# Two-layer graph network in float32: a written instruction order for four engines in layer 1, four memory pools, and gates in the first pairs

## The chip, the cores and the metric

The kernel runs on one core of one Trainium2 chip. The core has five engines that run side by side, each with one instruction stream that it takes in order: PE (matrix multiply, with a separate row PEld for the loads of its stationary operand), DVE (vector), ACT (scalar and table functions), POOL (GpSimd) and SP (Sync, which here only issues transfers). Transfers run on 16 DMA engines. SBUF is the working memory of 128 partitions; PSUM holds the results of matmuls in eight banks of 128 x 512 float32.

The metric is the time of one execution on the device in microseconds (us), the median of repeated runs. Lower is better. All data and all matmuls are float32.

## The reference, cut to what matters

The input is 128 graphs of 128 nodes with 512 features (`x`), a dense weighted adjacency matrix for each graph, and a node mask.

```python
# layer 0
h = relu(layernorm(x))
Xw = h @ Wv + bv
sj, si = Xw @ aw[:d, 0], Xw @ aw[d:, 0]
e = leaky_relu(sj[:, None, :] + si[:, :, None] + ab, 0.2)
t = adj * exp(e);  t = t / (sum(t, -1) + 1e-12)
H = h @ Wk[0] + bk[0] + (t @ h) @ Wk[1] + bk[1] + (t @ t @ h) @ Wk[2] + bk[2]
x = x + relu(H)
# layer 1
h = relu(layernorm(x))
q, k = split(h @ Wqk);  v = h @ Wv1
agg = adj @ (k * mask)
w = mask / sqrt(512) * sum(q * agg, -1)
x = x + softmax(w, over the 128 nodes)[:, :, None] * v
```

## The kernel before

**Layer 0** goes over 64 pairs of graphs. The products with 512 x 512 weights are done by Strassen's scheme with seven instead of eight block products (`strassen`): a left operand in four blocks and four sums of them (`left_sums`, tile `sx`), a right operand prepared once (`combine`). For a pair p, `y10(p)` makes the products with the first two weights in banks a1, b1, c1, e1; `inner(p)` and `outer(p, z)` multiply by the transition matrix `t` (through a copy `zz`); `y2(p + 2)` makes the third product two pairs ahead in the other four banks. Beside them run, for other pairs, the layer norm (`norm0`, `norm2`, with a logarithm and an exponential on ACT and five small DVE operations that end in `rs`), the transposition of h through DRAM (`by_blocks`, `transposed`), and the attention (`attention`, which makes `z`, `t` and the transposed adjacency `aT`). For layer 1, `for_layer1` writes the transposed h to DRAM (`xd`), and `norm2`, `outer` and `attention` write h (`h2d`), x (`x1d`) and the adjacency (`atd`). In pairs 3 to 9, `prepare` makes layer 1's right factors and writes them to DRAM (`rwd`).

**Layer 1** goes over 32 quads of graphs (two pairs). q·agg is turned into h times one matrix, so that layer 1 needs a 512 x 1024 product of each node; it is done by Strassen's scheme twice over: an outer level with the seven factors 1 to 7, and in each of them an inner level of seven products, 49 products of 128 x 128 by 128 x 256 for a quad. The left factors of the outer level are tile `f`: four blocks loaded from `xd` (`load_left`), three of which are also summed, and four sums on POOL. The inner sums are tile `in`, made by DVE (`inner_sums`: first 0 to 3 of the factors, then the last three). `one_round` makes the seven products of one to three factors in a set of four banks; its seven steps p1, p5, p6, p2, p7, p3, p4 depend on one another through ACT's copies between banks. A quad is two calls of `together`, each with one round in set 1 and one in set 2: factors 1, 5 and 2, 6 in the first, 3, 7 and 4 in the second. Between the two, `aggregate` multiplies the adjacency (`at`) by h into banks a1, a2, e1, e2, and ACT copies the result to `agg`.

The results go to tile `c` (four blocks of a quad, three buffers) through `plain_ends` and `adding_ends`; an adding end has a DVE add from PSUM into `s` and a POOL add from `s` into `c` (L737). Two wider POOL adds (128 x 1024, L832 in the middle and L851 at the end of a quad) finish the outer level. Then `scores` multiplies `agg` by one block of `c` and sums (DVE, L795); `spread_scores` sends the scores through DRAM so that every partition has them (`pwt`, `pwd`, `pw`); one quad later `peaks`, `exps` and `factors` make the softmax and `scale` (ACT, L83) applies it; and two quads later `store` adds x with an accumulating transfer on the POOL queue (`c<-x1d`, L805) and writes the output on the Sync queue (L806).

**What sets the order.** The program is traced as Python; a scheduler then orders the instructions of each engine by priority and by its own estimate of when they can start, and places the waits. `tc.issue_after(ins)` puts what is traced in its block behind `ins` on the engine of `ins`; `behind(name, op, ...)` does that with the last instruction kept under a name in `done`. In the kernel before, PE's order is written out fully (`ordered`), and a few others are tied to such names. A tile that takes the memory of an older one waits until its readers are done; pools opened later take the memory of pools that were closed. At the change of layers the pools of layer 0 are closed, and one pool (`back`) takes their place:

```python
    layer0.close()

    back = ctx.enter_context(tc.tile_pool(name="back", bufs=1))
    fpools[1] = back
    C, W, PW, S = {}, {}, {}, {}
```

The first quad's h, adjacency and last three right factors are then loaded by ACT's queue (`load_rest(0, nc.scalar)` and L670). In a quad, the loads of the next h and adjacency (`load_rest`, L663 and L664) are traced after the stores of two quads ago, and the loads of the left factors for two quads ahead (`load_left`, L618) at the end of the quad.

Of the kernel before, what the change touches and what calls it, by code (L numbers as in the profile page):

```python
# [15 lines left out]
def kernel(  # L16
# [25 lines left out]
    nc = tc.nc  # L42
# [25 lines left out]
    loads = layer0.enter_context(tc.tile_pool(name="loads", bufs=4))  # L68
    front = layer0.enter_context(tc.tile_pool(name="front", bufs=2))
# [261 lines left out]
    def left_sums(hT):  # L331
# [3 lines left out]
        s = front.tile([P, 4, HC * N], FP, name="sx", bufs=3)  # L335
# [7 lines left out]
    def strassen(banks, left, right, s, first, ends, steps={}):  # L343
# [20 lines left out]
        done["u2"] = nc.scalar.copy(c, b).ins  # L364
# [15 lines left out]
    def begin(p):  # L380
        hT = front.tile([P, G, DC, N], FP, name="x", bufs=3)
        transposed(HV.pop(p), hT)
        LEFT[p] = left_sums(hT)
# [33 lines left out]
    def attention(p):  # L417
# [6 lines left out]
        nc.scalar.activation(z, z, AF.Exp)  # L424
# [37 lines left out]
    def y10(p, steps):  # L462
# [3 lines left out]
        def end12(b, t):  # L466
# [6 lines left out]
            (1, 0): lambda c: None}, steps)  # L473
# [48 lines left out]
    hT0 = front.tile([P, G, DC, N], FP, name="x", bufs=3)  # L522
# [28 lines left out]
    for p in range(NP):  # L551
        def lefts():
            if p == 0:
                behind("t", norm0, 2)
                behind("rs", begin, 1)
                return
            if p + 2 < NP:
                behind("t", begin, p + 2)
            if p + 3 < NP:
                behind("left", norm0, p + 3)  # L560
# [3 lines left out]
        y10(p, {1: lefts, 6: lambda: t_transposed(p)})  # L564
# [8 lines left out]
        if p == 0:  # L573
            begin(2)
            norm0(3)
# [13 lines left out]
        if p == 2:  # L589
            rightl = combine({(kh, k): rl[:, kh * HC:(kh + 1) * HC, k] for kh in range(2)  # L590
                              for k in range(2)}, [tl[:, i] for i in range(4)])
        if 3 <= p < 3 + len(FACTORS):
            prepare(FACTORS[p - 3], stage)
# [19 lines left out]
    def load_left(q, pool):  # L613
        f = F[q] = pool.tile([P, 8, G, HC, N], FP, name="f")
        fv = f.rearrange("p o j k n -> p o (j k n)")
        for o, p, kh in ((1, 2 * q, 0), (2, 2 * q, 1), (L21, 2 * q + 1, 0), (4, 2 * q + 1, 1)):
            at = L21 if o == L21 else SLOT[o]
            nc.sync.dma_start(fv[:, at], XD[p][kh].rearrange("p g n -> p (g n)"))  # L618
        at = {o: fv[:, i] for o, i in SLOT.items()}
        nc.gpsimd.tensor_add(at[5], fv[:, L21], at[4])  # L620
        nc.gpsimd.tensor_sub(at[6], at[5], at[1])  # L621
        nc.gpsimd.tensor_sub(at[3], at[2], at[6])
        nc.gpsimd.tensor_sub(at[7], at[1], fv[:, L21])  # L623

    def inner_sums(q, pool, first, n):

        v = F[q][:, first:first + n]
        s = pool.tile([P, 4, n, N], FP, name=f"in{first}")
        b = {(j, k): v[:, :, j, k] for j in range(G) for k in range(2)}
        nc.vector.tensor_add(s[:, 0], b[1, 0], b[1, 1])  # L630
        nc.vector.tensor_sub(s[:, 1], s[:, 0], b[0, 0])
        nc.vector.tensor_sub(s[:, 2], b[0, 0], b[1, 0])
        nc.vector.tensor_sub(s[:, 3], b[0, 1], s[:, 1])
        for i in range(n):
            IN[q, FACTORS[first + i]] = s[:, :, i]

# [6 lines left out]
    fpools = [early, None]  # L643
    load_left(0, early)
    inner_sums(0, early, 0, 4)
    layer0.close()

    back = ctx.enter_context(tc.tile_pool(name="back", bufs=1))
    fpools[1] = back
    C, W, PW, S = {}, {}, {}, {}  # L650

    def begin_quad(q):

        S[q] = [back.tile([P, 2, D], FP, name=f"s{i}", bufs=1) for i in (1, 2)]
        C[q] = back.tile([P, 4, G, 2, HD], FP, name="c", bufs=3)
        W[q] = wcols[q % 3]

    def load_rest(q, queue=nc.sync):
        H2[q] = back.tile([P, 2, G, D], FP, name="h2", bufs=2)
        AT[q] = back.tile([P, 2, G, N], FP, name="at", bufs=2)  # L660
        for i in range(2):
            p = 2 * q + i
            queue.dma_start(H2[q][:, i], H2D[p].rearrange("g n d -> n g d"))  # L663
            queue.dma_start(AT[q][:, i], ATD[p])  # L664

    load_rest(0, nc.scalar)
    begin_quad(0)
    for o in FACTORS[4:]:
        RW[o] = back.tile([P, 7, HD], FP, name=f"rw{o}")
        nc.scalar.dma_start(RW[o], RWD[o])  # L670

    def copy(to, at):
        done["copy"] = nc.scalar.copy(to, at).ins  # L673
# [46 lines left out]
    def plain_ends(to):  # L720

        return {(0, 0): lambda a: copy(to(0, 0), a),
                (1, 1): lambda e, t: nc.vector.tensor_add(to(1, 1), e, t),
                (0, 1): lambda b, t: nc.vector.tensor_add(to(0, 1), b, t),
                (1, 0): lambda c: copy(to(1, 0), c)}

    def adding_ends(to, other, engine=nc.gpsimd):

        def one(i, j):
            def end(a):  # L730
                done["end"] = nc.vector.tensor_add(to(i, j), a, other(i, j)).ins  # L731
            return end

        def two(i, j):
            def end(e, t):
                nc.vector.tensor_add(t, e, t)  # L736
                engine.tensor_add(to(i, j), t, other(i, j))  # L737
# [14 lines left out]
    def peaks(w, pw):  # L752
# [4 lines left out]
        nc.vector.tensor_reduce(peak, pw, AX.X, OP.max, negate=True)  # L757
        return w, pw, peak

    def exps(w, pw, peak, at, graphs):  # L760
        for j in graphs:
            ej = back.tile([P, N], FP, name="ej", bufs=2)
            behind("copy", nc.scalar.activation, ej, pw[:, j, :], AF.Exp,
                   bias=peak[:, j:j + 1], accum_out=w[:, 2, at + j:at + j + 1])

    def factors(w, pw, peak, at):
        v = w[:, :, at:at + pw.shape[1]]
        nc.vector.tensor_add(v[:, 3], v[:, 0], peak)
        behind("copy", nc.scalar.activation, v[:, 4], v[:, 3], AF.Exp)
        nc.vector.reciprocal(v[:, 5], v[:, 2])  # L770
        nc.vector.tensor_mul(v[:, 3], v[:, 4], v[:, 5])
# [198 lines left out]
```

## Time and profile before

| | before |
|---|---|
| median of 3 runs | 2424.51 us (2423.55 to 2425.39) |
| span of the profiled execution | 2428.1 us |
| mean granted PE clock | 0.982 |
| one pair of layer 0, steady (start to start of the same matmul) | 22.08 us |
| layer 0 ends, layer 1's first matmul | 1484.6 us |
| first and last L832 (31 of them, one in each quad but the last) | 1521.4 and 2376.4 us |
| `c<-x1d`, issue to landing, median | 6.7 us |
| `f<-xd`, issue to landing, median | 4.9 us |

How to read it: a busy share is an average over stages with different limits. The span is cut into 40 slices of 60.7 us; a digit is the busy share of an engine in tenths. A wait is written as the engine and the line that waited, then what released it. Lines of a helper stand for all that call it: L88 is every matmul, L83 everything issued through `behind`, L673 ACT's copies in layer 1.

### The profile page before, as it was taken

Reading aid. Unit: us, or ns where it says so; the run is one execution under the profiler, and the core shown is the slowest. Engines: PE = TensorE matmul, PEld = TensorE weight load, DVE = VectorE, ACT = ScalarE, POOL = GpSimd, SP = SyncE. Lnnn points to the kernel's source line nnn. Section 1 sums busy time; section 2 is a strip of 40 time slices with the busy share of each in tenths; the row PEclk is TensorE's granted clock in tenths of the full one; section 3 lists DMA queues with packets and bytes.
Section 4 is the critical chain, followed back from the end, with each engine's and each line's share of the span. In section 5 each row is a group of like instructions: output and inputs, shape, how many; then the busy total and the mean of one; then the engine's idle time right before and its main releaser. Section 6 shows DMA issues by size and latency. Waiting matters only on the chain.

```text
span 2428.1 us, 29205 instructions
## 1 busy us (share of the span) xinstructions
PE 2285.2 (94%) x8227; PEld 1553.5 (64%) x8227; DVE 1710.4 (70%) x4210; ACT 1259.0 (52%) x2932; POOL 865.2 (36%) x844
## 2 busy tenths in 40 slices
PE   8899989999999999999999996998989988989896
PEld 4566656665666566656665664777777767777774
DVE  5666656766666666666666663988887888888887
ACT  3455545555555555555555553555555555555554
POOL 3011111211111111111111110777767777776664
PEclk9999999999999999999999998999999999999999
DMA  7566767666666666666666655366665655666665
GB/s 199 167 194 202 228 218 206 196 189 187 199 190 182 192 200 189 186 188 200 189 186 188 201 159 181 116 166 167 176 176 161 171 157 157 168 171 167 168 172 149
DMA packets 378768, 440.68 MB, mean 181 GB/s; under 512 B 35226, under 2 KB 233498, under 8 KB 378606
## 3 DMA queue, kind: packets, MB, share of 16 engines
q1 hardware_dynamic: 346236, 382.67, 50.1%
q0 software_dynamic: 30960, 51.82, 12.0%
q10 hardware_dynamic: 1410, 4.33, 0.5%
q8 instruction: 65, 1.06, 0.2%
q14 instruction: 97, 0.79, 0.1%
HBM read 256.07 MB, written 182.63 MB: 181 GB/s over the span
## 4 chain that ended last, share of the span: by engine, by line
PE 65%; DMA 10%; POOL 10%; DVE 6%; issue 4%; ACT 2%; SPq 2%; POOLq 0%; ACTq 0%; DVEq 0%
PE c L88 18%; PE a L88 18%; PE b L88 18%; PE e L88 10%; DMA f<-xd 5%; DMA c<-x1d 4%; POOL c L737 3%; POOL f L621 1%; POOL f L623 1%; POOL f L620 1%; DVE junk L795 1%; POOL c L832 1%; POOL c L851 1%; SPq L618 1%; DVE c L731 1%
## 5 line engine op out<-in xcount | busy, mean ns | idle before, releaser
L108 POOL DMA_DIRECT2D agb<-in_adj_dram x256 | 148.5, 587 | 785.5 <-DVE aT L436 721.9
L88 PE MATMUL a<-r,x 128*128 128x512 f32 (+1 forms) x1024 | 375.5, 489 | 8.1 <-DVE x L320 8.0
L88 PEld LDWEIGHTS a<-r,x 128*128 128x128 f32 x1024 | 190.4, 191 | 88.0 <-issue 62.5
L737 POOL TENSOR_TENSOR c<-s,c 128x512 f32<-128x512 f32 (+1 forms) x186 | 220.9, 1201 | 61.1 <-DVE s L736 54.6
L88 PE MATMUL b<-rw,in 128*128 128x256 f32 x896 | 227.3, 395 | 11.1 <-ACT b L673 11.1
L88 PE MATMUL a<-rw,f 128*128 128x256 f32 x896 | 217.0, 382 | 3.0 <-ACT agg L673 3.0
L88 PEld LDWEIGHTS b<-rw,in 128*128 128x128 f32 x896 | 177.2, 199 | 44.2 <-ACT b L673 18.1
L88 PEld LDWEIGHTS a<-rw,f 128*128 128x128 f32 x896 | 169.1, 190 | 43.4 <-issue 12.9
L88 PE MATMUL c<-t,x 128*128 128x257 f32 (+1 forms) x512 | 192.2, 498 | 2.0 <-ACT s L368 1.6
L88 PE MATMUL b<-t,sx 128*128 128x257 f32 (+1 forms) x512 | 191.7, 497 | 1.1 <-ACT b L360 1.1
L88 PE MATMUL c<-t,sx 128*128 128x257 f32 (+1 forms) x512 | 187.5, 488 | 0.0
L88 PE MATMUL e<-t,sx 128*128 128x257 f32 (+1 forms) x512 | 187.0, 488 | 0.0
L88 PE MATMUL b<-r,sx 128*128 128x257 f32 (+1 forms) x512 | 186.3, 486 | 0.0
L88 PE MATMUL c<-rw,in 128*128 128x256 f32 x448 | 118.9, 408 | 68.1 <-ACT c L673 68.1
L320 DVE STREAM_TRANSPOSE x<-hv 128x512 f32<-128x512 f32 x254 | 165.3, 688 | 13.4 <-DMA hv<-h2d 8.7
L276 DVE BATCH_NORM_STATS2 st<-xg 128x6 f32<-128x512 f32 x128 | 82.4, 685 | 116.4 <-DMA xg<-in_x_dram 116.4
L795 DVE SCALAR_TENSOR_TENSOR junk<-agg,wscale,c 128x512 f32<-128x512 f32 x128 | 160.1, 1251 | 3.6 <-POOL c L737 2.3
L630 DVE TENSOR_TENSOR in<-f 128x512 f32<-128x512 f32 x64 | 53.5, 836 | 140.1 <-POOL f L621 137.5
L368 ACT COPY s<-c 128x257 f32<-128x257 f32 (+1 forms) x128 | 60.6, 473 | 171.0 <-PE c L88 171.0
L88 PEld LDWEIGHTS c<-t,x 128*128 128x128 f32 x512 | 92.3, 189 | 84.9 <-issue 50.2
L88 PEld LDWEIGHTS b<-t,sx 128*128 128x128 f32 x512 | 94.0, 191 | 81.6 <-issue 61.0
L88 PEld LDWEIGHTS c<-rw,in 128*128 128x128 f32 x448 | 86.3, 198 | 90.8 <-ACT c L673 79.3
(216 smaller groups left out, 4718.5 us busy)
## 6 DMA issues: line engine op xcount, KB each, us to landing
x1d<-x SPq DMA_DIRECT2D x64, 512.0 KB, 3.7
h2d<-h SPq DMA_DIRECT2D x64, 512.0 KB, 3.1
hv<-h2d SPq DMA_DIRECT2D x256, 128.0 KB, 3.6
xd<-x SPq DMA_DIRECT2D x128, 256.0 KB, 3.0
f<-xd SPq DMA_DIRECT2D x128, 256.0 KB, 4.9
xg<-in_x_dram SPq DMA_DIRECT2D x63, 512.0 KB, 4.5
hd<-h SPq DMA_DIRECT2D x63, 512.0 KB, 3.1
hv<-hd SPq DMA_DIRECT2D x252, 128.0 KB, 2.9
```

What stands on the lines that cost most here:

```text
L88: done["mm"] = op(*args, **how).ins
L108: nc.gpsimd.dma_start(agb[p][c * S32:(c + 1) * S32].rearrange("p g q i -> p (g q) i"), v[c])
L276: nc.vector.bn_stats(st, src[:, j, :])
L320: nc.vector.transpose(dst[:, j].rearrange("p f (n b) -> p f n b", n=Q), hv[:, j].rearrange("p n (f a) -> p f n a", f=Q))
L368: nc.scalar.copy(s[:, 1], c)
L618: nc.sync.dma_start(fv[:, at], XD[p][kh].rearrange("p g n -> p (g n)"))
L620: nc.gpsimd.tensor_add(at[5], fv[:, L21], at[4])
L621: nc.gpsimd.tensor_sub(at[6], at[5], at[1])
L623: nc.gpsimd.tensor_sub(at[7], at[1], fv[:, L21])
L630: nc.vector.tensor_add(s[:, 0], b[1, 0], b[1, 1])
L737: engine.tensor_add(to(i, j), t, other(i, j))
L795: nc.vector.scalar_tensor_tensor(junk, agg[:, pair, j], wscale[:, b:b + 1], y[:, j].rearrange("p h d -> p (h d)"), op0=OP.mult, op1=OP.mul ...
```

## The change

In layer 1, every instruction of Sync, POOL, DVE and ACT goes through `put`, which ties it behind the one before it on its engine; so the order in which the Python code traces them is the order in which each engine takes them. The code is then rearranged by hand. `load_left` is split in two: the loads (for the next quad, at its head, in `catch_up`) and POOL's sums (`sum_left`, in the first half of the quad before their use). `inner_sums` becomes four steps that are hung between PE's steps. The last adds, the scores and their spread move from a quad's end to the head of the next one (`catch_up`). `store` is split into the accumulating transfer (`add_x1`) and the write. `exp_own`, the exponential of the scores on a row's own partition, leaves `factors` and goes ahead of the others.

The pool `back` becomes four, so that each takes memory of layer 0 that is freed at another time; in layer 0 the tiles `x` and `sx` get a pool of their own (`lefts`). The first h, adjacency, right factors and second quad's left factors are loaded by the POOL queue instead of ACT's. In the first pairs, `norm0(3)`, `combine` of the right factor and `prepare` are put behind the last DVE operation of `outer`, and pair 0's copy c<-b of `y10` behind the exponential of `attention`.

```diff
+    lefts = layer0.enter_context(tc.tile_pool(name="lefts", bufs=3))
...
-        s = front.tile([P, 4, HC * N], FP, name="sx", bufs=3)
+        s = lefts.tile([P, 4, HC * N], FP, name="sx")
...
-        done["u2"] = nc.scalar.copy(c, b).ins
+        behind(u2, nc.scalar.copy, c, b)
...
-        nc.scalar.activation(z, z, AF.Exp)
+        done["z"] = nc.scalar.activation(z, z, AF.Exp).ins
...
-            (1, 0): lambda c: None}, steps)
+            (1, 0): lambda c: None}, steps, "warm" if p else "z")
...
-            norm0(3)
+            behind("x1", norm0, 3)
...
-            rightl = combine({(kh, k): rl[:, kh * HC:(kh + 1) * HC, k] for kh in range(2)
+            rightl = behind("x1", combine, {(kh, k): rl[:, kh * HC:(kh + 1) * HC, k] for kh in range(2)
...
-            prepare(FACTORS[p - 3], stage)
+            behind("x1", prepare, FACTORS[p - 3], stage)
...
+    def put(engine, op, *args, **how):
+
+        if engine in done:
+            with tc.issue_after(done[engine]):
+                done[engine] = op(*args, **how).ins
+        else:
+            done[engine] = op(*args, **how).ins
...
-    back = ctx.enter_context(tc.tile_pool(name="back", bufs=1))
+    back = [ctx.enter_context(tc.tile_pool(name=f"back{i}", bufs=1)) for i in range(4)]
...
-    load_rest(0, nc.scalar)
-    begin_quad(0)
-    for o in FACTORS[4:]:
-        RW[o] = back.tile([P, 7, HD], FP, name=f"rw{o}")
-        nc.scalar.dma_start(RW[o], RWD[o])
+    begin_quad(0)
+    load_rest(0, swdge)
+    for o in FACTORS[4:]:
+        RW[o] = back[1].tile([P, 7, HD], FP, name=f"rw{o}")
+        swdge(RW[o], RWD[o])
+    load_left(1, back[2], swdge)
...
+    def catch_up(q):
+
+        if q + 1 < NQ:
+            load_left(q + 1, back[2] if q % 2 == 0 else early, sync)
+
+        pool(nc.gpsimd.tensor_add, outer(q - 1, 1), outer(q - 1, 3), outer(q - 1, 1))
+        scores(q - 1, 1, C[q - 1][:, 2])
+        PW[q - 1] = spread_scores(W[q - 1])
+        if q > 1:
+            add_x1(q - 2, 0)
...
-                 {5: lambda: scale(q - 2, 1, 0), 6: lambda: scale(q - 2, 1, 1)} if q > 1 else {})
-
-        done["v"] = nc.gpsimd.tensor_add(outer[0], outer[3], outer[1]).ins
-        if q > 1:
-            behind("v", store, q - 2)
-        if q > 0:
-            late = behind("end", peaks, W[q - 1], PW.pop(q - 1)) + (0,)
-        agg = aggregate(q)
-        load_rest(q + 1)
-        inner_sums(q + 1, early, 0, 4)
+                 {0: work(*sums[:2]), 1: work(*sums[2:], lambda: sum_left(q + 1)),
+                  2: lambda: load_rest(q + 1, sync),
+                  3: (lambda: scale(late, 1, 0)) if q > 1 else nothing,
+                  5: (lambda: scale(late, 1, 1)) if q > 1 else nothing})
+        if q > 1:
+            store(late, 0)
+        if q > 0:
+            soft = peaks(W[prior], PW.pop(prior))
+
+        pool(nc.gpsimd.tensor_add, outer(q, 0), outer(q, 3), outer(q, 1))
+        if q > 1:
+            add_x1(late, 1)
+        aggregate(q)
         scores(q, 0, c[:, 2])
-
-        work = {i: lambda i=i: exps(*late, (i,)) for i in range(4)}
-        work[4] = lambda: factors(*late)
-        work.update({i: lambda i=i: scale(q - 1, 0, i - 5) for i in (5, 6)})
+        sums = inner_sums(q + 1, early, 0, 4)
+
+        hooks = {0: sums[:2], 1: sums[2:]}
+        if q > 0:
+            hooks = {0: [lambda: exp_own(*soft), lambda: exp(*soft, 0)] + sums[:2],
+                     1: [lambda: exp(*soft, 1)] + sums[2:],
...
-        nc.gpsimd.tensor_add(outer[1], outer[3], outer[1])
-        if q + 2 < NQ:
-            load_left(q + 2, fpools[q % 2])
-        inner_sums(q + 1, back, 4, 3)
-        scores(q, 1, c[:, 2])
-        PW[q] = spread_scores(W[q])
+        if q > 1:
+            store(late, 1)
+            C.pop(late)
```

## The prediction

> **What bounds the kernel now.** I read the busy line and the slices first, then the busy times by stage, then the chain of waits in layer 1, then the waits by total, and last the timeline of one quad.
>
> ```profile
> PE 2285.2 (94%) x8227; PEld 1553.5 (64%) x8227; DVE 1710.4 (70%) x4210; ACT 1259.0 (52%) x2932; POOL 865.2 (36%) x844
> ...
> PE   8899989999999999999999996998989988989896
> ...
> POOL 3011111211111111111111110777767777776664
> ```
>
> The 94% says "TensorE-bound", and for slices 3 to 24 (layer 0) that is right: a pair costs 22.08 us, all of it matmuls. The last 16 slices (layer 1) are another stage: PE falls below 90% and POOL rises from 1 to 7 tenths.
>
> ```profile
> core 0: us, PE busy (x) PEld busy (x) DVE busy (x) ACT busy (x) POOL busy (x), PEclk, DMA share, GB/s
> 1521.40:2376.40 855.00, 776.45 (x3206) 615.85 (x3204) 712.39 (x1046) 461.96 (x1045) 604.98 (x417) 0.98 0.60 163
> 1484.60:1521.40 36.80, 18.30 (x66) 13.62 (x65) 15.62 (x30) 8.78 (x17) 8.05 (x6) 0.72 0.68 246
> ```
>
> The first window runs from the first to the last of the 31 POOL adds of L832, one in each quad: 855.0/30 = 28.5 us per quad. DVE is busy 23.7 of it, POOL 20.2, ACT 15.4. A quad has 98 matmul records of 0.216 us (eight take 1.73) and 8 of 0.43: PE needs 24.6. So 3.9 us per quad are lost. The second window is the change of layers: PE worked 18.3 of 36.8 us.
>
> The chain of waits (start, length, what) repeats one loop from quad to quad:
>
> ```profile
> 1601.53 2.67 POOL c L832
> 1604.90 8.08 DMA c<-x1d
> 1616.30 4.98 DMA f<-xd
> 1630.10 2.68 POOL c L832
> ```
>
> The waits of layer 1 (total, times, longest) show how it reaches PE, and those of the Sync queue where it starts:
>
> ```profile
> POOL f L623 <- DMA f<-xd: 151.4, 23, 8.2
> DVE in L630 <- POOL f L621: 128.4, 28, 6.1
> ACT ej L83 <- DVE peak L757: 94.5, 29, 4.6
> ...
> PE c L88 <- ACT c L673: 65.3, 27, 3.7
> ...
> SPq L806 <- DMA c<-x1d: 455.3, 56, 15.7
> ```
>
> Read upwards: PE waits for a copy in ACT's queue, queued behind an exponential that waits for the peak, which DVE does after a sum that waited for POOL, which waited for the left factors `f`; their load stood in the Sync queue behind stores that wait for the accumulating transfer `c<-x1d`. One quad of POOL's timeline (start, length, and in brackets the idle time before it):
>
> ```profile
> 1802.80 2.68 POOL L832 TENSOR_TENSOR c<-c 128x1024 f32<-128x1024 f32 x1
> 1805.42 2.44 POOL L805 DMA_DIRECT2D c<-x1d  x2
> ...
> 1822.55 1.26 POOL L623 TENSOR_TENSOR f<-f 128x512 f32<-128x512 f32 x1 [6.37 <-DMA f<-xd]
> ...
> 1828.21 2.94 POOL L737 TENSOR_TENSOR c<-s,c 128x512 f32<-128x512 f32 x2
> 1831.22 2.67 POOL L832 TENSOR_TENSOR c<-c 128x1024 f32<-128x1024 f32 x1
> ```
>
> With the `f` loads issued at 1816.52 (Sync's row of the same timeline), the loop is: L832 2.6, from the x1d issue to the f issue 11.1, to the first f sum 6.0, four f sums 5.7, two L737 3.0: 28.4 us. That is the period. No engine is full; a loop through a DMA queue sets the pace.
>
> **What the Trainium skill says.** "SBUF — State Buffer", section "Who interferes with whom": a DVE instruction with two SBUF inputs and a GpSimd instruction that reads SBUF exclude each other; the later one blocks fully. The trace agrees: a 384-wide sum (L632), 0.55 us alone, took 2.70 at 1842.33, beside a POOL add of 2.66. "Perfetto Trace Analysis", section "GPSIMD Engine Instruction": GpSimd spans are unreliable, starts are to be used; hence my POOL lengths are from starts (f sums 1822.55, 1823.78, 1825.12, 1826.47). "DMA: Bandwidth & Descriptors", section "Issuing engines are not separate DMA queues": another issuing engine adds no bandwidth; at the change of layers the transfers already ran at 246 GB/s. "TensorE: Matmul & The Clock Gate", section "What's actually happening": an idle PE falls to half clock; after the 18.5 us pause there, eight matmuls took 3.78 us instead of 1.89.
>
> **The change part by part.**
>
> (1) Written order on Sync, POOL, DVE and ACT in layer 1. The four `f` loads now stand at the head of a quad. In the instruction order they still follow the second store of the quad before, which waits for its own accumulating transfer; but that is now one transfer, issued right after L832's add, and the loads of h and at no longer stand between. New loop: add 2.6, one x1d (median 6.7 from issue to landing), store issue 0.4, f issue to sum 6.0, f sums 5.7, two c adds 3.0: 24.4 us, an estimate. The old loop loses 4 us and falls to PE's 24.6.
>
> (2) What the order costs. DVE work per quad, by starts: ten 512-wide adds from PSUM at 0.6, four 256-wide at 0.36, four 384-wide sums at 0.5, four 512-wide at 0.6, four scores at 0.78, one reduction 0.6, transpose and small ones 0.7: 16.2 us. Waits in the new fixed order: the scores of pair 1 head DVE's queue at the quad's start, and wait for POOL's last c adds and then for the lock behind the 1024-wide add (L851's): 3.4. Behind them queue the spread of the scores, the 384-wide sums and the PSUM add that frees bank a2 for the aggregate. The scores of pair 0 meet the other 1024-wide add: 2.6. The factor product 0.7. The f sums, moved to the first half, run when the 384-wide sums do: nothing if f lands late, up to 4.8 if each of four sums waits for an f sum. That makes 22.9 to 27.7. Laid out in time: if f lands about 9.5 us into the quad, there is no collision, but POOL's c adds and then the scores come later, and the quad closes at 25.7; if it lands at 6.8, all four collide, DVE frees a2 some 1.5 us late, and it closes at 27.1. The scores' spread takes 7.4 us through DRAM and is back before the peak in both. I take 26.3: 2.2 us less than 28.5, times 30 quads = 66 us. Ends: 24.9 (PE with a little waiting) and 27.7.
>
> (3) ACT: exponentials now wait for a peak that DVE reaches 2 to 4 us earlier; `exp_own` moves up, which costs nothing (0.2 us, beside matmuls). ACT has 7.9 us in PE's 9.1 of the second half (four pairs of copies at 0.95, four exponentials at 0.6, two scalings at 0.73, `exp_own` 0.2), so it hides.
>
> (4) Four pools, and the first h, at and right factors by the POOL queue. Before, ACT's queue issued them and stood 19.7 us behind `h<-h2d`, which waited for layer 0's last `xd<-x`, with PE's copies behind it: PE paused 18.5 us. Now ACT has nothing to issue, and the memory of the first tiles was last read at pair 63's matmuls. But 2.7 MB of right factors, 1 MB of f and 1.3 MB of h and at must come in some 17 us, and POOL sums the second quad's f before the first quad's adds, for which ACT's second-half copy into `s` waits: I leave 5 us of new pause, and gain 12 (8 to 18).
>
> (5) Gates in the first pairs. In pairs 10, 11 and 12 (26.5, 26.4 and 25.0 us instead of 22.1) ACT has the copy of zz before the logarithm of the next norm, and DVE's add into bank e waits 5 us. In the new order only pair 10 is put right: 4.4. Pair 0's exponential moves ahead of the c copy (PE waited 3.4 for t), and the 1024-wide `combine` leaves the front of x of pair 2 (PE waited 8.0), though norms now stand there: 2.6 together. From pair 13 to the end of layer 0 no engine's order changes. Sum 7 (3 to 12).
>
> (6) The last quads: stores moved behind the work, exponentials spread out: 2. The `lefts` pool only renames memory in layer 0: nothing.
>
> Sum: 66 + 12 + 7 + 2 = 87; 2424.5 - 87 = 2337.5.
>
> **The rivals.** A: PE becomes the bound. For it: both loops can reach 24.6, and with fewer pauses the clock stays full. 24.9 per quad: 30 x 3.6 = 108, with 21 elsewhere 2295. Against it: POOL's 16.6 us of adds (8 at 1.25, 2 at 0.7, 2 at 2.6) and DVE's 7.6 us of work with two SBUF inputs (sums 4.4, scores 3.1, product 0.15) exclude each other, 24.2 us on one port. B: the lock takes the place of the load. All collisions happen: 27.7, 24 + 21 = 45 less, 2380. C: slower. A fixed order leaves no other work to fill a wait: if peaks also come 1.5 late behind the spread, 29.2 per quad, 21 lost, and the gain at the boundaries is used up by transfers that are late there: 2432.
>
> **How the numbers follow.** My forecast (25.5 to 27.2 per quad) 0.46, A 0.20, B 0.22, C 0.10, no difference 0.02. The range reaches from just below A to a quad of 28.4 with the other gains: 2290 to 2402. Faster 0.88 (forecast, A, B), same 0.02, slower 0.10.
>
> **What would show it.** Right: the period of L832's successor near 26.3; POOL's wait for f below 3 us a quad; Sync's wait for x1d still there but before f no more than 2 us; pauses of PE at the aggregate's second matmul instead of at product 7; PE's pause at the change of layers under 7 us; pair 10 at 22.1 us. Wrong: ACT's copies still the releaser of product 7 by over 2 us, POOL still waiting 5 us for f, or PE without pauses in layer 1.

## The result and the profile after

The changed kernel takes 2362.53 us in the median (2354.90 to 2370.35), against 2424.03 us; the ratio is 0.9746, with a 95% interval of 0.9713 to 0.9779. It is 61.5 us faster. Forecast were 87 us.

The page of the changed kernel, busy line and slices:

```profile
PE 2259.0 (96%) x8227; PEld 1540.4 (65%) x8227; DVE 1758.6 (75%) x4210; ACT 1258.4 (53%) x2932; POOL 838.1 (36%) x855
...
PE   8899999999999999999999999899999999999996
...
DVE  5576666766666666666666665699999999999997
POOL 3011111211111111111111111477776777767772
```

PE's slices of layer 1 are now nines, but so are DVE's. The busy times of two stretches (same columns as before), from the first to the last of the 31 POOL adds that stand where L832 stood, and the first two quads:

```profile
1497.30:2304.00 806.70, 754.07 (x3162) 600.60 (x3163) 763.43 (x1051) 458.45 (x1035) 574.07 (x417) 0.99 0.66 174
1470.57:1534.51 63.94, 54.63 (x213) 42.76 (x212) 42.41 (x69) 26.09 (x57) 32.17 (x27) 0.89 0.53 177
```

The quad takes 806.70/30 = 26.9 us instead of 28.5. DVE is busy 763.43/30 = 25.4 of them, though it has no work that it hadn't before (23.7). The waits of layer 1 (total, times, longest):

```profile
PEld a L89 <- DVE c L618: 76.1, 31, 3.2
PE a L89 <- DVE c L618: 39.2, 24, 2.4
DVE junk L618 <- POOL c L618: 39.1, 32, 13.6
...
PE c L89 <- ACT c L618: 0.9, 2, 0.5
...
POOL f L618 <- DMA f<-xd: 0.2, 1, 0.2
```

(Most instructions of layer 1 now bear L618, the line of `put`, so that tiles tell them apart.) POOL's wait for `f`, 151.4 us before, is gone; so is nearly all of PE's wait for ACT at product 7 (65.3 us before). A new wait stands in their place: PE's bank `a` waits for a DVE add. One quad of DVE's timeline shows what DVE does at that time:

```profile
1913.33 2.82 DVE L618 SCALAR_TENSOR_TENSOR junk<-agg,wscale,c 128x512 f32<-128x512 f32 x1 [0.79 <-POOL c L618]
...
1916.20 2.40 DVE L618 SCALAR_TENSOR_TENSOR junk<-agg,wscale,c 128x512 f32<-128x512 f32 x1
...
1918.78 1.37 DVE L618 TENSOR_TENSOR in<-f 128x384 f32<-128x384 f32 x1
1920.18 1.51 DVE L618 TENSOR_TENSOR in<-in,f 128x384 f32<-128x384 f32 x1
1921.61 1.61 DVE L618 TENSOR_TENSOR in<-f 128x384 f32<-128x384 f32 x1
1923.15 0.55 DVE L618 TENSOR_TENSOR in<-f,in 128x384 f32<-128x384 f32 x1
1923.62 0.68 DVE L618 TENSOR_TENSOR c<-a,c 128x512 f32<-128x512 f32 x1
```

And POOL and PE in the same time:

```profile
1913.26 2.35 POOL L618 TENSOR_TENSOR c<-c 128x1024 f32<-128x1024 f32 x1
...
1916.33 6.48 POOL L618 TENSOR_TENSOR f<-f 128x512 f32<-128x512 f32 x4
...
1924.35 1.12 PE L89 MATMUL a<-h,at 128*128 128x512 f32 x2 [2.21 <-DVE c L618]
```

The first score is blocked by the 1024-wide add, the second and three of the four 384-wide sums by POOL's `f` sums; the fourth sum runs alone and takes 0.55. (In 15 of the quads 2 to 29 the fourth is blocked too; the mean of all these sums is 1.40.) Only then comes the add from bank a2 (`c<-a,c`), and the aggregate's second matmul, which writes a2, has waited 2.2 us.

PE's idle time in quads 2 to 29 changes its place as well: 2.7 us a quad before, 2.3 of it at product 7 of the second half; 1.7 us now, nearly all at the aggregate's second matmul.

By stage, between the first matmuls of pairs and quads in the two profiles (us; pairs are counted from 0, as in the kernel and in the prediction):

| stage | before | changed | difference |
|---|---|---|---|
| up to pair 2 | 114.7 | 104.1 | -10.6 |
| pairs 2 to 8 | 154.9 | 156.4 | +1.5 |
| pairs 9 to 11 | 75.4 | 69.4 | -6.0 |
| pair 12 to the end of layer 0 | 1139.9 | 1140.6 | +0.8 |
| quads 0 and 1 | 70.5 | 63.9 | -6.6 |
| quads 2 to 29, each | 28.50 | 26.82 | -47.1 for 28 |
| quads 30, 31, end | 74.8 | 74.3 | -0.5 |

They add up to 68.5, 7 more than the medians give: the profiled execution of the kernel before took 2429.84 us, 5.8 more than its median, and that of the changed kernel 2361.39, 1.1 less. A part lies in the first row: in the profiles of experiments 7 and 8, whose layer 0 is that of before, pair 2 starts at 111.7 and 113.7 us, not at 114.7.

### The profile page after: what moved, and what is told of

Same layout as the page of the kernel before. It is cut to its first block, busy times and chain, and to the rows that moved or that the text cites. A ratio compares the mean times of both kernels' runs of the same rounds, so it can differ in the third digit from the quotient of the medians.

```text
span 2359.6 us, 29167 instructions
## 1 busy us (share of the span) xinstructions
PE 2259.0 (96%) x8227; PEld 1540.4 (65%) x8227; DVE 1758.6 (75%) x4210; ACT 1258.4 (53%) x2932; POOL 838.1 (36%) x855
## 4 chain that ended last, share of the span: by engine, by line
PE 78%; DVE 11%; DMA 4%; issue 3%; ACT 2%; POOL 2%; SPq 0%; DVEq 0%; ACTq 0%; POOLq 0%
PE a L89 23%; PE b L89 21%; PE c L89 21%; PE e L89 13%; DVE junk L618 3%; DVE in L618 2%; DVE c L618 2%; POOL c L618 1%; DVE s L618 1%; DMA pwd<-pwt 1%; DMA pw<-pwd 1%; ACT h L295 1%; DMA f<-xd 1%; DVE wcol L618 1%; DMA t<-in_L_gnn_Wv_dram 1%
## 5 line engine op out<-in xcount | busy, mean ns | idle before, releaser
L618 POOL TENSOR_TENSOR c<-s,c 128x512 f32<-128x512 f32 (+1 forms) x186 | 199.9, 1088 | 230.3 <-DVE s L618 225.4
L618 DVE SCALAR_TENSOR_TENSOR junk<-agg,wscale,c 128x512 f32<-128x512 f32 x128 | 245.8, 1920 | 44.2 <-POOL c L618 39.1
L89 PE MATMUL b<-rw,in 128*128 128x256 f32 x896 | 219.8, 385 | 0.9 <-ACT b L618 0.9
L618 POOL TENSOR_TENSOR f<-f 128x512 f32<-128x512 f32 x127 | 194.5, 1541 | 18.9 <-DMA f<-xd 13.9
L89 PEld LDWEIGHTS b<-rw,in 128*128 128x128 f32 x896 | 170.2, 192 | 29.1 <-ACT b L618 6.4
L369 ACT COPY s<-c 128x257 f32<-128x257 f32 (+1 forms) x128 | 60.6, 474 | 175.9 <-PE c L89 175.8
L618 POOL TENSOR_TENSOR c<-c 128x1024 f32<-128x1024 f32 x62 | 145.8, 2351 | 2.4
L89 PEld LDWEIGHTS e<-t,sx 128*128 128x128 f32 x512 | 97.5, 190 | 68.6 <-issue 60.0
```

The lines of the kernel that those rows point to most:

```text
L89: done["mm"] = op(*args, **how).ins
L369: nc.scalar.copy(s[:, 1], c)
L618: done[engine] = op(*args, **how).ins
```

## The experiments

**Theory and rivals.** L: what is left per quad is PE waiting for DVE's add from a2, queued behind two-input instructions that POOL blocks; another order gives most of it back. M: DVE and POOL together fill the shared port, so any order costs the same. And of the kernel before: the loop through Sync's queue (theory), or the port (rival).

**1. The sums later.** In the changed kernel, the four 384-wide sums after the last PSUM add of the first half:

```diff
-                 {0: work(*sums[:2]), 1: work(*sums[2:], lambda: sum_left(q + 1)),
+                 {1: lambda: sum_left(q + 1),
...
-                  5: (lambda: scale(late, 1, 1)) if q > 1 else nothing})
+                  5: (lambda: scale(late, 1, 1)) if q > 1 else nothing,
+                  6: work(*sums)})
```

> The changed kernel with one move in DVE's order: the four 384-wide sums of a quad's second-half factors no longer stand between the scores' transpose and the add that frees bank a2, but after the last PSUM add of the first half. POOL's order is as it was. Theory L (what is left per quad is PE waiting for DVE's add from a2, queued behind sums that are blocked by POOL's f sums): the pause of 2 to 3 us at the aggregate's second matmul goes, the sums take 0.55 us instead of 1.4, the quad falls from 26.9 to 24.8-25.5 us, in all 2305 to 2325 us. Rival M (DVE and POOL have no slack on the shared port, so whatever is moved collides elsewhere): the quad stays at 26.3 to 27.0 and the pause moves to the second half's product 5, which reads these sums; 2350 to 2365 us.

Measured: 2339.22 us, ratio 0.9645 (0.9623 to 0.9666), 26.1 us a quad. The aggregate no longer waits, but PE now waits 1.3 us a quad at product 7 of the second half. DVE's timeline of this run:

```profile
1880.84 1.45 DVE L618 TENSOR_TENSOR in<-f 128x384 f32<-128x384 f32 x1
1882.32 1.51 DVE L618 TENSOR_TENSOR in<-in,f 128x384 f32<-128x384 f32 x1
1883.75 2.70 DVE L618 TENSOR_TENSOR in<-f 128x384 f32<-128x384 f32 x1
1886.37 0.55 DVE L618 TENSOR_TENSOR in<-f,in 128x384 f32<-128x384 f32 x1
1886.84 0.67 DVE L618 TENSOR_REDUCE peak<-pw 128x4 f32<-128x512 f32 x1
```

They now meet POOL's c adds and the other 1024-wide add, and the peak, on which ACT's exponentials wait, stands behind them. Neither expectation held: 0.7 of the 1.4 to 2.1 us that L wanted were won, and M's collision came as well, though at product 7 and not at the product 5 that M named.

**2. Quad 0's order on POOL.** The `f` sums of quad 1 behind quad 0's adds, in quad 0 alone:

```diff
-                 {0: work(*sums[:2]), 1: work(*sums[2:], lambda: sum_left(q + 1)),
+                 {0: work(*sums[:2]), 1: work(*sums[2:], *([lambda: sum_left(q + 1)] if q else [])),
...
         pool(nc.gpsimd.tensor_add, outer(q, 0), outer(q, 3), outer(q, 1))
+        if q == 0:
+            sum_left(1)
```

What it mends, in the timelines of the changed kernel (POOL, then PE):

```profile
1475.40 0.54 POOL L618 DMA_DIRECT2D f<-xd  x1 [0.73 <-DMA h<-h2d]
1489.62 5.16 POOL L618 TENSOR_TENSOR f<-f 128x512 f32<-128x512 f32 x4 [13.68 <-DMA f<-xd]
1494.74 2.48 POOL L618 TENSOR_TENSOR c<-s,c 128x512 f32<-128x512 f32 x2
...
1498.17 2.93 PE L89 MATMUL c<-rw,in 128*128 128x256 f32 x6 [6.74 <-ACT c L618]
```

> The changed kernel with one move in POOL's order, in quad 0 alone: the four f sums of quad 1 stand behind quad 0's two c adds and its 1024-wide add, not ahead of them. Theory: the pause of 6.7 us at product 7 of quad 0's second half and the half clock after it come from POOL waiting 13.7 us for f's fourth load with the c adds queued behind; the pause goes and the change of layers is 6 to 8 us shorter: 2354 to 2357 us. Rival: the loads of h, at, right factors and f on POOL's DMA queue are what is late, and PE then waits for f's sums at the start of quad 1 instead: gain of 0 to 3 us, 2360 us.

Measured: 2355.14 us, ratio 0.9706 (0.9688 to 0.9724): 7.4 less than the changed kernel, though the two intervals overlap a little (that of the changed kernel begins at 0.9713). In the profiles quads 0 and 1 take 53.8 us instead of 63.9. The pause at product 7 is gone; one of 3.4 us at the start of quad 1, behind DVE's sums of the late `f`, is what the rival saw. The theory holds for the larger part: the pause was made by the order, with work queued behind one load.

**3. Without the gates of layer 0.**

```diff
-        behind(u2, nc.scalar.copy, c, b)
+        done["u2"] = nc.scalar.copy(c, b).ins
...
-            behind("x1", norm0, 3)
+            norm0(3)
...
-            rightl = behind("x1", combine, {
+            rightl = combine({
...
-            behind("x1", prepare, FACTORS[p - 3], stage)
+            prepare(FACTORS[p - 3], stage)
```

> The changed kernel without the gates in layer 0's first pairs (norms, the right factors' combination and their preparation free again, pair 0's c copy not behind the exponential); layer 1 as changed. Theory: pairs 10 and 11 go back to 26.2 to 26.7 us (they are 22.5 and 24.4 with the gates), pairs 3 to 10 gain back 0.2 each: 4 to 7 us longer, 2367 to 2370 us. Rival: the 14.3 us by which the profile of the changed kernel leads at the end of layer 0 all come from the gates: 12 to 14 us longer, 2375 us.

Measured: 2371.70 us, ratio 0.9781 (0.9763 to 0.9798), 9.2 more than with the gates; here too the intervals overlap. In the profiles pair 12 starts at 337.2 us instead of 329.9: 4.3 of these 7.3 us come before pair 2, 4.5 in pairs 10 and 11 (25.0 and 26.4 us, with the gates 22.5 and 24.4), and 1.5 go back in pairs 2 to 8, which are slower with the gates (22.3 us instead of 22.1). That is between the two expectations, nearer the first. In the kernel before, pair 12 starts at 345.0 (341.9 and 344.0 in the two kernels below that have its layer 0); so 4.7 to 7.8 us ahead of pair 12 are not the gates'. How much of that is the spread of single executions is not known; of the change only the `lefts` pool is left there, and it was not tried alone.

**4. Only Sync's order kept.**

```diff
-        if engine in done:
+        if engine in done and engine == "sync":
```

> The changed kernel with the written order of layer 1 kept on Sync's queue alone; DVE, ACT and POOL are in the order that the scheduler gives them. Theory (the gain per quad came from the f loads ahead of stores and of h and at): POOL's wait for f stays under 1 us a quad and the quad stays at or under 27.5 us: 2340 to 2385 us. Rival (the orders of DVE, ACT and POOL are what shortened the quad): the quad is back at 28 us or over, 2400 us or over, although f is there in time.

Measured: 2637.29 us, ratio 1.0870 (1.0842 to 1.0897), 36.5 us a quad: far worse than either expected. ACT and PE in one of its quads (L620 is `put` here):

```profile
1909.14 0.58 ACT L620 COPY s<-c 128x512 f32<-128x512 f32 x1 [0.85 <-PE c L89]
1918.20 0.40 ACT L620 ACTIVATE ej<-pw,peak 128x128 f32<-128x128 f32 x1 [8.48 <-DVE peak L620]
...
1918.60 0.56 ACT L620 COPY s<-c 128x512 f32<-128x512 f32 x1
```

```profile
1919.22 2.07 PE L89 MATMUL c<-rw,f 128*128 128x256 f32 x4 [6.72 <-ACT s L620]
```

The scheduler's order on ACT has an exponential ahead of the last copy that PE needs in the first half. The exponential waits for the peak (254 us in 28 quads), the peak for the spread of the scores through DRAM (107 us), and PE for the copy: 7.3 us a quad. In the kernel before, ties of `behind` keep the peak and the exponentials back; the changed kernel has no such ties, since `put` does their work, so this run is not the order of the kernel before on three engines. POOL's wait for `f` is 15.5 us in all, as the theory has it, and doesn't help: the quad is set elsewhere. What the other three orders are worth in time, against those of the kernel before, this run does not tell.

**5. The f sums on DVE.** `sum_left` with `dve(nc.vector...)` instead of `pool(nc.gpsimd...)`, put after the adds that free banks a and e:

```diff
-                 {0: work(*sums[:2]), 1: work(*sums[2:], lambda: sum_left(q + 1)),
+                 {0: work(*sums[:2]), 1: work(*sums[2:]),
...
+                  4: (lambda: sum_left(q + 1)) if q else nothing,
```

> The changed kernel with the four f sums of a quad on DVE instead of POOL: after the first adds that free the banks a and e in the first half (in quad 0 at the start of its second half). POOL then has 13.5 us of work a quad instead of 18.6, and DVE four adds of 0.7 us more. Theory L (POOL's f sums block DVE's sums and second score, and so hold back the add that frees bank a2): the four 384-wide sums take 0.55 us instead of 1.4, the aggregate's second matmul does not wait, and with quad 0's wait for f gone too the time is 30 x 1.6 + 6 lower, 2300 to 2318 us. Rival M (DVE is the fuller engine, and 2.8 us of work more on it cost what the lock gives back): the quad stays at 26.3 to 27.2 us, 2345 to 2370 us.

Measured: 2336.44 us, ratio 0.9633 (0.9619 to 0.9647), 26.4 us a quad. The lock is as L has it: the 384-wide sums take 0.54 us in the mean instead of 1.40, and PE no longer waits for DVE's add from a2. The time fits neither expectation. 8.4 of the 26 us won against the changed kernel come from quads 0 and 1 (55.5 us instead of 63.9); in the other quads DVE's further work delays what ACT waits for (ACT's own exponential waits 47.9 us in all for DVE, 3.2 in the changed kernel), and PE waits for ACT:

```profile
PE c L89 <- ACT c L618: 25.0, 15, 2.0
...
PE a L89 <- DVE c L618: 2.3, 6, 0.7
```

**6. Sync's order given up, the other three kept.**

```diff
-        if engine in done:
+        if engine in done and engine != "sync":
```

> The changed kernel with the written order kept on DVE, ACT and POOL and given up on Sync's queue, where the scheduler's own order has one out store between the two loads that spread the scores, and the h and at loads and the other store ahead of the f loads, as in the kernel before. Theory (the f loads ahead of h and at are what shortens the quad): POOL waits for f again, 1 to 4 us a quad, and the quad is at 27.5 to 29 us: 2385 to 2430 us. Rival (with the order of the accumulating transfers on POOL changed, Sync's order is worth little): 26.7 to 27.2 us a quad, 2360 to 2372 us.

Measured: 2327.95 us, ratio 0.9595 (0.9579 to 0.9611): both expectations wrong, and 35 us less than the changed kernel. POOL does wait for `f` again, but only 32 us in all, and the quad is at 25.7. POOL and DVE in one of its quads:

```profile
1896.65 2.35 POOL L618 TENSOR_TENSOR c<-c 128x1024 f32<-128x1024 f32 x1
...
1901.22 5.87 POOL L618 TENSOR_TENSOR f<-f 128x512 f32<-128x512 f32 x4 [1.09 <-DMA f<-xd]
```

```profile
1899.60 0.75 DVE L618 SCALAR_TENSOR_TENSOR junk<-agg,wscale,c 128x512 f32<-128x512 f32 x1
...
1900.53 0.52 DVE L618 TENSOR_TENSOR in<-f 128x384 f32<-128x384 f32 x1
1901.08 0.56 DVE L618 TENSOR_TENSOR in<-in,f 128x384 f32<-128x384 f32 x1
1901.55 1.63 DVE L618 TENSOR_TENSOR in<-f 128x384 f32<-128x384 f32 x1
...
1904.65 0.68 DVE L618 TENSOR_TENSOR c<-a,c 128x512 f32<-128x512 f32 x1
```

The `f` sums start 4.6 us after the 1024-wide add, not 3.1 (these are the medians of quads 2 to 29 too). In that gap DVE has the second score and two sums unblocked, and the add from a2 comes 8.0 us after the 1024-wide add starts instead of 10.4 (in the medians 8.0 and 9.9). PE's wait at the aggregate falls from 1.7 to 0.1 us a quad; 0.6 us at product 7 take its place. The gap also varies within this run: one quad with 3.5 us waits 1.1 us at the aggregate, four with 4.2 or 4.3 us wait 0.3 there, those with 4.5 or more not at all, and two with 6.2 and 6.3 us wait 1.5 us at product 7 instead (quads 2 and 25, the shortest ones, don't fit: 3.1 and 6.4 us, and hardly a wait). So here a later load makes the quad shorter, up to a point. But Sync's order moved stores, h and at too, and the 1024-wide add itself starts 0.6 us earlier in the quad (3.7 us after its first matmul, not 4.3); these were not separated.

**7. The kernel before with its stores behind the loads.** `store` is split; the accumulating transfers stay where they were, the two out stores are issued behind the last `f` load of the quad:

```diff
-            behind("v", store, q - 2)
+            behind("v", add_x1, q - 2)
...
             load_left(q + 2, fpools[q % 2])
+        if q > 1:
+            behind("f", put_out, q - 2)
```

> The kernel before, with one edit: the two out stores of a quad stand behind the four f loads in Sync's queue, not ahead of two h and at loads and of f. Nothing else of the change. Theory (the period of 28.5 us is the loop L832, x1d transfer, store, f load, f sums): the wait of f for x1d goes, POOL's wait for f (5 us a quad) falls under 1, and the quad is 25.3 to 26.8 us: 2325 to 2375 us. Rival (f late is a symptom; DVE and POOL exclude each other and set the period): 28.0 us or more a quad, 2405 us or more.

Measured: 2319.94 us, ratio 0.9560 (0.9541 to 0.9579). One edit to the kernel before brings 104 us, 43 more than the whole change. Its quads 2 to 29 (columns as above):

```profile
1552.70:2251.10 698.40, 694.46 (x2969) 561.72 (x2968) 669.06 (x980) 433.10 (x980) 578.78 (x392) 1.00 0.68 189
```

698.4/28 = 24.94 us a quad, and PE is busy in 694.5 of 698.4. Sync's queue, two lines of its timeline, and POOL's wait for `f`:

```profile
1852.77 1.84 SPq L618 DMA_DIRECT2D f<-xd  x4
1854.72 1.24 SPq L817 DMA_DIRECT2D out_dram<-c  x2
```

```profile
POOL f L623 <- DMA f<-xd: 1.4, 5, 0.4
```

With the stores behind the loads, the quad falls below what was expected, to PE. The edit leaves one other cause open: the scheduler, placing DVE's instructions anew, now has the third 512-wide sum (L632) behind the peak and not ahead of it, and in Sync's queue h and at too are free of the stores. The kernel before itself decides this. In its quad 2 no store stands ahead of the `f` loads yet, since the first one is issued at 1580.83 us, while DVE has its old order (L632, then the peak):

```profile
1555.57 1.74 SPq L618 DMA_DIRECT2D f<-xd  x4
```

```profile
1558.31 2.67 POOL L851 TENSOR_TENSOR c<-c 128x1024 f32<-128x1024 f32 x1
1560.93 1.58 POOL L623 TENSOR_TENSOR f<-f 128x512 f32<-128x512 f32 x1
```

POOL does not wait, and this quad takes 24.6 us; in the quads after it, with the stores ahead of the loads, the `f` sums come 8 to 11 us after that add instead of 2.6, and the quad takes 26.3 to 31.2 us. So the loop named in the prediction is what held the kernel before. The port does not prevent it: in this run too the 384-wide sums are blocked (1.49 us in the mean), but ahead of the scores, in the time in which DVE would wait for POOL's c adds.

**8. The kernel before with the first loads on POOL's queue.**

```diff
-    load_rest(0, nc.scalar)
+    load_rest(0, nc.gpsimd)
...
-        nc.scalar.dma_start(RW[o], RWD[o])
+        nc.gpsimd.dma_start(RW[o], RWD[o])
```

> The kernel before, with one edit: the first h and at tiles and the right factors of layer 1 are loaded by POOL's queue instead of ACT's; the memory pool stays one. Theory (ACT's copies were queued behind those issues): the pause of 18.5 us at product 7 of quad 0 falls below 10 us, quad 0 from 45.9 to 33-39 us, 2411 to 2418 us. Rival (what is late is the memory under the tiles, which one pool frees only after layer 0's last reader, so that the four pools and not the queue are what helped): PE waits as long, at the aggregate or at f's sums: 2420 to 2426 us.

Measured: 2426.71 us, ratio 1.0014 (1.0000 to 1.0028): nothing won, as the rival has it. PE's pauses in this run:

```profile
1503.54 3.78 PE L88 MATMUL c<-rw,f 128*128 128x256 f32 x8 [8.99 <-ACT s L673]
1510.73 3.19 PE L88 MATMUL a<-h,at 128*128 128x512 f32 x4 [3.42 <-issue]
...
1518.51 0.70 PE L88 MATMUL a<-rw,f 128*128 128x256 f32 x2 [1.88 <-DMA rw<-rwd]
1521.43 1.08 PE L88 MATMUL a<-rw,f 128*128 128x256 f32 x2 [2.22 <-DMA rw<-rwd]
```

Most of the 18.5 us is only spread out: 9.0 + 3.4 + 1.9 + 2.2 = 16.5, and quads 0 and 1 together take 72.0 us, 70.5 before. ACT's own copy into `s` still waits for layer 0's last `xd<-x`. That fits the rival, memory that one pool frees late; the queue alone changes nothing. That the four pools alone, with ACT's queue, would do was not tried.

**9 and 10. The sums first, and with quad 0's order.** In the changed kernel, DVE's order as the scheduler has it in experiment 7: the 384-wide sums at the head of the quad, before the scores.

```diff
             begin_quad(q)
+            for step in inner_sums(q, back[0], 4, 3):
+                step()
             catch_up(q)
-            sums = inner_sums(q, back[0], 4, 3)
+            sums = []
```

> The changed kernel with one move in DVE's order: the four 384-wide sums of a quad stand at its head, before the two scores of the quad before, not behind them. Sync, POOL and ACT as changed. Theory O (in the changed order DVE first waits for POOL's c adds with the scores at its head, and meets POOL's f sums with the sums; the order, not the amount of work, is what costs): the sums run while POOL does its c adds, the add that frees bank a2 is done 3 to 4 us earlier, the aggregate's pause goes, 25.0 to 25.8 us a quad, 2310 to 2332 us. Rival M (the shared port is full, so the sums and scores are only blocked by other POOL instructions): 26.3 to 26.9 us a quad, 2345 to 2363 us.

> The move of the sums to the head of the quad together with quad 0's order on POOL (c adds ahead of the f sums of quad 1). If the two costs are separate, 7 us below the first alone: 2303 to 2325 us. If quad 1 then waits for f, equal to it.

Measured: 2328.92 us, ratio 0.9612 (0.9596 to 0.9627), and 2323.66 us, 0.9593 (0.9571 to 0.9616). The quad is at 25.9 in both, and theory O holds in time (2310 to 2332) though the quad is just over its 25.8. The sums are blocked as before (0.97 and 2.70 us for two of them), but in time that DVE had spent waiting; that is 1 us a quad from order alone. Quad 0's order takes 8.3 us off quads 0 and 1 in the profiles (53.9 instead of 62.2); in the medians it is 5 us, and the two intervals overlap. PE's remaining waits are 0.7 us a quad at product 7 and 0.2 to 0.3 at the aggregate.

**11. The exponentials one product later**, on top of 10:

```diff
-            hooks = {0: [lambda: exp_own(*soft), lambda: exp(*soft, 0)] + sums[:2],
-                     1: [lambda: exp(*soft, 1)] + sums[2:],
-                     2: [lambda: exp(*soft, 2)],
-                     3: [lambda: exp(*soft, 3)],
+            hooks = {0: sums[:2],
+                     1: [lambda: exp_own(*soft), lambda: exp(*soft, 0)] + sums[2:],
+                     2: [lambda: exp(*soft, 1)],
+                     3: [lambda: exp(*soft, 2), lambda: exp(*soft, 3)],
```

> The two moves of the run before (sums at the head of the quad, quad 0's order) and one in ACT's order: the own exponential and the four others stand one product later in the second half, behind the copies of e, so that no copy which PE needs stands behind a wait for the peak. Theory A (what is left per quad, 25.9 against 24.9 in the kernel before with its stores moved, is ACT's written order: 0.66 us of PE's wait for ACT's copies at product 7): the wait goes and the quad is at 25.0 to 25.4 us, 2300 to 2312 us. Rival: the scores' spread arrives late (DVE waits 3 us for it) and the exponentials, moved back, push the factors and the scalings of c later, so that the copies of the next quad wait instead: 25.8 to 26.2 us a quad, 2320 to 2332 us.

Measured: 2321.84 us, ratio 0.9567 (0.9543 to 0.9591), 25.6 us a quad. The wait at product 7 falls from 0.67 to 0.06 us, but 0.26 us at product 6, which waits for ACT's copy into bank b, come in its place, as the rival said, and the time is not told apart from that of 10. What else separates 25.6 from 24.9 stays open.

**12. The best of both.** Experiment 7, and of the change only the gates, the `lefts` pool and the four memory pools with the first loads on POOL's queue; layer 1 in the scheduler's order.

```diff
-    back = ctx.enter_context(tc.tile_pool(name="back", bufs=1))
+    back = [ctx.enter_context(tc.tile_pool(name=f"back{i}", bufs=1)) for i in range(4)]
...
-    load_rest(0, nc.scalar)
     begin_quad(0)
+    load_rest(0, nc.gpsimd)
```

> The kernel before with the stores behind the f loads, and of the change only the gates in the first pairs and the four memory pools with h, at and the right factors on POOL's queue; no written order in layer 1. Stores alone gave 2319.9; the gates are worth 9 us by their own run; the boundary was 63 us over two quads in the changed kernel with quad 0's order mended to 54, and 70.5 with stores alone: 2319.9 - 9 - 7 to 16 = 2295 to 2304 us. Rival (without the written order the scheduler puts POOL's f sums of quad 1 ahead of quad 0's adds, and nothing is won at the boundary): 2308 to 2313 us.

Measured: 2301.94 us (2298.40 to 2305.20), ratio 0.9501 (0.9480 to 0.9522), 60.6 less than the changed kernel and within the expected range. The quad is at 24.88, quads 0 and 1 at 57.6 (70.5 in experiment 7); a pause of 5.7 us at product 7 of quad 0 is left, behind POOL's sums of quad 1's `f`, as the rival said, but it does not use up the gain.

## Why the prediction was right, and where it was not

**The loop** (step 1) was right. POOL's wait for `f` fell from 151.4 to 0.2 us in layer 1, and experiment 7 with quad 2 of the kernel before shows that this loop held the kernel before: 28.5 to 24.9 us a quad by moving two stores. Its new length was right too. In one quad of the changed kernel, from one middle add to the next (Sync, then POOL):

```profile
1897.35 12.54 SPq L618 DMA_DIRECT2D out_dram<-c  x2
1910.01 2.47 SPq L618 DMA_DIRECT2D f<-xd  x4
```

```profile
1901.01 2.35 POOL L618 TENSOR_TENSOR c<-c 128x1024 f32<-128x1024 f32 x1
...
1925.57 2.50 POOL L618 TENSOR_TENSOR c<-s,c 128x512 f32<-128x512 f32 x2 [2.76 <-DVE s L618]
1928.15 2.35 POOL L618 TENSOR_TENSOR c<-c 128x1024 f32<-128x1024 f32 x1
```

The adds are 27.1 us apart, and POOL spends 2.8 of it waiting for DVE: 24.4 us without that wait, the figure of step 1. One sign failed: `f` was to wait for x1d no more than 2 us, but its loads are still issued right behind a store that waits for x1d up to 12 us (306.5 us in all). It costs nothing, because POOL's sums of `f` now stand behind another add.

**The DVE order** (step 2) named the right wait, at the right instruction: the scores behind POOL's add, the sums behind the `f` sums, the aggregate's second matmul at the end. Its size was wrong, and it is the term that failed. The prediction had two layouts, 25.7 if `f` comes late and 27.1 if it comes early enough to collide, and took 26.3 between them. But step 1's loop, 24.4 us, is shorter than either layout's quad, so by step 1 the quad does not wait for `f`. Measured 26.82, with three or four of four sums blocked; over 30 quads this is 16 us of the 25 that were missing. So the colliding layout was good to 0.3 us. That experiment 6, with `f` later, is at 25.68 looks as good for the other layout, but is partly luck: the layout had `f` 9.5 us into the quad and no collision, and there the sums start at 8.4 us in the median and two of four are still blocked. Rival A (PE's bound) needs only another order: experiment 7. Rival C's figure, 2432, does not follow from its terms: 2424.5 + 21 - 7 - 2 is 2436.5 without the gain at the change of layers.

**ACT** (step 3) hides in the changed kernel: PE waits 0.9 us in all for its c copies. It is the next to show: as soon as DVE's add is early, product 7 waits for it (1.3, 0.9, 0.6 and 0.7 us a quad in experiments 1, 5, 6 and 9).

**The change of layers** (step 4) was to bring 12, and brought 6.6. Its cause was named, POOL's `f` sums ahead of the c adds, and sized at a pause of 5 us. The pause was 6.7; after it matmuls ran at half clock (six took 2.93 us instead of 1.46); and quad 1 waits for DVE's add like the others, which the 5 us had left out. With POOL's order mended (experiment 2), quads 0 and 1 are 10 us shorter in the profile, 7.4 in the medians. That ACT's issues were what held PE before is refuted as the sole cause by experiment 8.

**The gates** (step 5) came out at 7.3 against 7 forecast, by the profiles of experiment 3 and the changed kernel. That the sum agrees is luck, since the parts differ: 4.5 in pairs 10 and 11 (4.4 forecast, for pair 10 alone, which gains 2.5), 4.3 instead of 2.6 at the start, and 1.5 lost in pairs 2 to 8, which was not foreseen. The other 7.0 us that layer 0 gains between the two profiles were not forecast: the `lefts` pool was put at nothing, and whether it or the spread of single executions makes them stays open. **The tail** (step 6) brought 0.5 instead of 2.

The sum by stage with the gates' share alone is 47.1 + 6.6 + 7.3 + 0.5 = 61.5. That this is the difference of the medians is chance, as the 7.0 us are left out of it. The mechanism was right; of the 25 us that are missing, 16 are step 2's term, 5 step 4's and 1.5 the tail's.

## What to carry to other kernels

When no engine is full, find the loop that sets the period, and first move the one instruction that closes it: two stores behind four loads brought 104 us, where a written order of four engines with the same aim brought 61 together with everything else. A quad that lacks the instruction under suspicion, as quad 2 lacks the stores, is a test that the kernel makes by itself. A written order also freezes which instructions of DVE and POOL meet and block each other; put the two-input DVE work into the time in which DVE would wait for POOL anyway, and not behind that wait. And when an estimate has two layouts, decide between them from its own earlier steps instead of taking the middle.

## What was not expected of the hardware

A load that lands earlier can cost time: with POOL's `f` sums 1.5 us nearer to its 1024-wide add they meet DVE's second score and sums, and the quad was 1.1 us longer (26.82 against 25.68 in experiment 6, with what else differs there). It is not the landing as such: in quads 2 and 11 of the changed kernel POOL's add starts 2.8 us into the quad instead of 4.3 and the `f` sums at 5.9 and 6.0 instead of 7.4, and these quads take 25.0 us. All four sums are blocked there too, but the add from a2 is reached 12.6 us into the quad instead of 14.1, and PE waits 0.2 us at the aggregate. What counts is how late DVE is for PE's next use of the bank.

Short waits of PE cost more than their length. Over quads 2 to 29 the records have PE's clock at half for 37.5 us in the kernel before, 10.2 in the changed one and 0 in experiment 7, whose longest pause of PE there is 0.7 us. Each stretch is 3.4 us long and follows a single pause of 2.1 to 3.7 us. In the changed kernel ten of these quads pause 2.2 us at the aggregate: three of them, each with such a stretch, take 28.8 us, and the other seven 27.15. In the kernel before the half clock costs 0.7 us a quad, an estimate (37.5/2/28), beyond the waits that the profile lists.

The fourth `f` load on POOL's queue, behind 4.8 MB of others issued there within 8 us (h and at 1.3, right factors 2.75, f 0.77), let POOL wait until 14.2 us after its issue; on Sync's queue the median of these loads is 4.1 us. Most of this is not the queue: in experiment 12 these four loads stand on Sync's queue, at nearly the same time and with the same h, at and right factors in transfer, and the last of them lands 12.0 us after its issue, against 14.1 on POOL's in the changed kernel.
